# One fp32 product to a PSUM bank, wider token blocks and a shared weight ring in a mixture-of-experts stage

## The chip, the cores and the metric

The kernel runs on one NeuronCore of a Trainium2 chip. The metric is the device time of one execution in microseconds (us): the median of 3 runs before the change is 9032.1 us (9029.27 to 9032.78). The profile is of one execution that took 9036.42 us, of which 9034.7 us are the span between the first and the last instruction.

## The reference

Everything is fp32. A cross-attention of 4 x 1024 rows against 1024 columns comes first and takes the first 540 us; the change does not touch it. The rest is a mixture of experts over 4096 tokens of 1024 numbers, with 8 experts, each token going to two of them:

```python
topk_w, topk_idx = jax.lax.top_k(router_probs, TOP_K)          # TOP_K = 2
topk_w = topk_w / jnp.sum(topk_w, axis=-1, keepdims=True)
...
h = jax.lax.ragged_dot(x_rep_sort, w1, group_sizes)            # 1024 -> 3584
h = jax.nn.silu(h) * jax.lax.ragged_dot(x_rep_sort, w3, group_sizes)
out_sort = jax.lax.ragged_dot(h, w2, group_sizes)              # 3584 -> 1024
...
out = jnp.einsum('tkd,tk->td', out_rep, topk_w)
```

The router of the reference, evaluated on its inputs, sends 984, 991, 1080, 994, 1047, 1004, 1046 and 1046 tokens to the eight experts, 8192 in all.

## The kernel before, in words

The tokens of an expert are worked off in a *run* (`run`, L750) of `blocks` blocks of `width` tokens. The list RUNS (L22) has the allowed pairs; for each expert the smallest one that holds its tokens is chosen on the chip, and a loop over runs (L852) jumps through a switch to the code built for that pair. Here the eight runs are three blocks of 328 (once), 336 (three times), 352 (three times) and 360 tokens (once), 24 blocks and 8256 token places.

Every matrix product is one level of a Strassen-Winograd scheme: weights and tokens are cut in 2 x 2 quarters, and seven products p1 to p7 of half size replace eight. With n = width / 2, each product is a chain of matmuls with a 128 x 128 stationary weight and n moving columns, accumulated in PSUM. On an fp32 matmul TensorE executes two instructions, so two records in the profile are one matmul of the code. The seven products need sums of weight quarters (`weight_sums`, L580: four VectorE operations L585 to L588 on every loaded weight tile) and sums of token quarters ("factors").

- **First and second product** (w1 and w3, L769 to L797): 14 steps i2, each with a round of 28 matmuls for w1 and one for w3 (L781). After a round `combine` (L610) reads the seven results from PSUM on ScalarE and VectorE; then SiLU, the product of the two, and `token_sums` (L598), which makes the token factors of the third product once and keeps all seven in the tile `g` (14 x 7 x n).
- **Third product** (w2, L809 to L834): four quarters q of the 1024 output columns; in each, 14 steps of seven matmuls (L820). Weights come in four tiles of 8, 8, 6 and 6 rows of 128 (W2K). The seven results are combined, transposed back to token rows (`tokens_out`, L723, tile pt_y), scaled and added into `acc`, which holds rows gathered from the output; after the fourth quarter GpSimd scatters `acc` to the output with an indirect DMA (L736). The last block's fourth quarter is finished in the next run (`leftover`).
- **The next block's tokens** are gathered to `rows` by GpSimd (`load_rows`, L681), and transposed to `x` by TensorE in steps (`tokens_in`, L693, tile pt_h, copied from PSUM by ScalarE and VectorE in turn).

The steps of `tokens_in` and `tokens_out` stand in a list `late`, from which one is taken at fixed places between the matmuls. PSUM has eight banks of 512 fp32 columns: two products of n columns share a bank (BANK, L592), seven products take four banks, six banks serve them in turn, and two serve the transposes. Weight tiles are taken in turn from a pool of three (`wp`); the first two of the next run have buffers of their own, `w1a` and `w3a` with sums `s1a` (L661 to L663), loaded at the start of the last block's third product (`load_first`, L687).

TensorE executes in the order of the code (`manual_schedule`, L857). On the other engines a scheduler fixes the order when the program is built. Each engine, and SP (SyncE), which issues all the weight loads, works its own list strictly in order: an instruction that waits holds up everything behind it.

Of the kernel before, what the change touches and what calls it, by code (L numbers as in the profile page):

```python
# [18 lines left out]
P = 128  # L19
N = 512  # L20

RUNS = [(1, 192), (1, 376), (2, 288), (2, 376), (3, 288)]  # L22
RUNS += [(3, w) for w in range(320, 377, 8)]
# [10 lines left out]
def kernel(  # L34
# [493 lines left out]
    with ExitStack() as st:  # L528
        fst = st.enter_context(tc.tile_pool(name="fst", bufs=1))
        wp = st.enter_context(tc.tile_pool(name="wp", bufs=3))  # L530
        hp = st.enter_context(tc.tile_pool(name="hp", bufs=1))
        gp = st.enter_context(tc.tile_pool(name="gp", bufs=2))
        ip = st.enter_context(tc.tile_pool(name="ip", bufs=2))
        ps = st.enter_context(tc.tile_pool(name="ps", bufs=6, space=PSUM))
        pst = st.enter_context(tc.tile_pool(name="pst", bufs=2, space=PSUM))
# [4 lines left out]
        W2K = [8, 8, 6, 6]  # L540
        RT = 3
# [3 lines left out]
        XW = RT * P  # L545
        assert all(w // 2 <= NM and w <= XW for _, w in RUNS)


        T1, B11, B12, B21, B22, T2, T4 = range(7)
        T3 = B12  # L550
# [9 lines left out]
        def load(wf, ex, k0, kn, c0):  # L560
            t = wp.tile([P, KD, QW], F32, tag="w", name="wt")
            weights(t, wf, ex, k0, kn, c0)
            return t

        def factors(t, kn, halves, s):

            n = kn // 2
            if halves:
                v = t[:, :kn, :].rearrange("p (i h) c -> p i h c", h=2)
                lo, hi = v[:, :, 0, :], v[:, :, 1, :]  # L570
            else:
                lo, hi = t[:, :n, :], t[:, n:kn, :]
            s1, s2, s4 = (s[:, j, :n, :] for j in range(3))

            return dict(
                p1=lo[:, :, :P], p2=hi[:, :, :P], p3=s4, p4=hi[:, :, P:], p5=s1, p6=s2,
                p7=lo[:, :, P:],
            )

        def weight_sums(t, kn, halves, s=None):  # L580
            if s is None:
                s = wp.tile([P, 3, HK, P], F32, tag="s", name="ws")
            f = factors(t, kn, halves, s)
# [4 lines left out]
            nc.vector.tensor_tensor(a21, a11, a21, ALU.subtract)  # L588
            return f

        RIGHT = dict(p1=B11, p2=B21, p3=B22, p4=T4, p5=T1, p6=T2, p7=T3)
        BANK = dict(p1=(0, 0), p2=(1, 0), p6=(1, 1), p5=(2, 0), p7=(2, 1), p3=(3, 0), p4=(3, 1))  # L592
        ENDS = ["p1", "p6", "p7", "p4"]
# [4 lines left out]
        def token_sums(v, n):  # L598

            def two(a, b):  # L600
                return v[..., a : b + 1 : b - a, :]

            nc.vector.tensor_tensor(two(T1, T3), two(B12, B22), two(B11, B12), ALU.subtract)
            nc.vector.tensor_tensor(v[..., T2, :], v[..., B22, :], v[..., T1, :], ALU.subtract)
            nc.vector.tensor_tensor(v[..., T4, :], v[..., B21, :], v[..., T2, :], ALU.subtract)

        def banks():
            return [ps.tile([P, N], F32, tag="ps", name=f"ps{i}") for i in range(4)]

        def combine(pp, n, c, wide):  # L610

            def pair(t):
                return t[:, : 2 * n].rearrange("p (a b) -> p a b", b=n)

            def twice(v):
# [3 lines left out]
            nc.scalar.copy(p1s, pp[0][:, :n])  # L619
            nc.vector.tensor_tensor(pair(c), pair(pp[1]), twice(p1s), ALU.add)  # L620
            vu = gp.tile([P, 2, n], F32, tag="vu", name="vu")
            nc.vector.tensor_tensor(vu, pair(pp[2]), twice(c[:, n : 2 * n]), ALU.add)  # L622
            mid = c[:, n : 2 * wide - n].rearrange("p (a b) -> p a b", b=wide - n)[:, :, :n]
            nc.vector.tensor_tensor(mid, pair(pp[3]), vu, ALU.add)  # L624
            nc.vector.tensor_tensor(  # L625
                c[:, wide + n : wide + 2 * n], pp[2][:, :n], vu[:, 1, :], ALU.add
            )

# [30 lines left out]
        rd0 = fst.tile([P, RT], I32, name="rd0")  # L659
        rows = [fst.tile([P, D], F32, name=f"rows{s}") for s in range(RT)]  # L660
        w1a = fst.tile([P, KD, QW], F32, name="w1a")  # L661
        w3a = fst.tile([P, KD, QW], F32, name="w3a")
        s1a = fst.tile([P, 3, HK, P], F32, name="s1a")  # L663
# [6 lines left out]
        acc = [fst.tile([P, D], F32, name=f"acc{s}") for s in range(RT)]  # L670
        for a in acc:
            nc.gpsimd.memset(a, 0.0)
# [8 lines left out]
        def load_rows(s0):  # L681
            load_ids(ids0, s0)
            where_from(rd0, ids0)
            for s in range(RT):
                gather(rows[s], h_d, rd0, s, P)

        def load_first(i):  # L687
            ex = expert(i)
            load_rows(first_slot(i))
            weights(w1a, w1f, ex, 0, KD, 0)  # L690
            weights(w3a, w3f, ex, 0, KD, 0)

        def tokens_in():  # L693


            def step(s, h):
                pt = pst.tile([P, N], F32, tag="pt", name="pt_h")
                for k in range(HK):
                    nc.tensor.transpose(  # L699
                        pt[:, ts(k, P)], rows[s][:, ts(HK * h + k, P)], ident  # L700
                    )
                src = pt.rearrange("p (a b) -> p a b", b=P)
                dst = x[:, ds(HK * h, HK), ts(s, P)]
                if h % 2:
                    nc.vector.tensor_copy(dst, src)
                else:
                    nc.scalar.copy(dst, src)
# [14 lines left out]

        def tokens_out(ids, split, q, y):  # L723
# [3 lines left out]
            def step(s, r):  # L727
                pt = pst.tile([P, N], F32, tag="pt", name="pt_y")
                for d in range(2):
                    nc.tensor.transpose(pt[:r, ts(d, P)], yv[:, d, ds(s * P, r)], ident)  # L730
                part = acc[s][:r, ts(q, QW)]
                nc.vector.scalar_tensor_tensor(
                    part, pt[:r, :QW], ids.bitcast(F32)[:r, s, 1:2], part, ALU.mult, ALU.add
                )
                if q == DQ - 1:
# [3 lines left out]
                        in_=acc[s][:r, :],  # L739
# [7 lines left out]
        def leftover():  # L747
            return tokens_out(ids1, [P] * RT, DQ - 1, y1)

        def run(i, ex, s0, blocks, width):  # L750
            n = width // 2
            split = [min(P, width - c) for c in range(0, width, P)]

# [9 lines left out]
            for b in range(blocks):  # L763
                ids, rd = take_ids()
                last = b == blocks - 1
                if not last:
                    load_rows(s0 + (b + 1) * width)
                g = hp.tile([P, NI, 7, n], F32, tag="g", name="g")
                for i2 in range(NI):  # L769
                    cs = []  # L770
                    for wf, wa, tag in ((w1f, w1a, "c1"), (w3f, w3a, "c3")):
                        t = load(wf, ex, 0, KD, i2 * QW) if b or i2 else wa
                        if t is w1a:
                            left = factors(w1a, KD, False, s1a)
                        else:
                            left = weight_sums(t, KD, False)
                        pp = banks()
                        for p in ORDER if b or i2 else EARLY:
                            bk, half = BANK[p]
                            for k in range(HK):  # L780
                                nc.tensor.matmul(  # L781
                                    pp[bk][:, ts(half, n)], left[p][:, k, :],
                                    right[p][:, k, :],
# [8 lines left out]
                    nc.scalar.activation(c1, c1, AF.Silu)  # L792
                    nc.vector.tensor_tensor(
                        g[:, i2, B11 : B22 + 1, :].rearrange("p a b -> p (a b)"), c1, c3,
                        ALU.mult,
                    )
                    token_sums(g[:, i2, :, :], n)  # L797

                if last:
                    load_first(i + 1)  # L800
# [6 lines left out]
                for s, r in enumerate(split):  # L807
                    gather(acc[s][:r, :], of, rd, s, r)
                for q in range(DQ):  # L809
                    pp = banks()  # L810
                    i2 = 0
                    for kn in W2K:
                        t = load(w2f, ex, 2 * i2, kn, q * QW)
                        left = weight_sums(t, kn, True)
                        for k in range(kn // 2):
                            for p in ORDER:
                                bk, half = BANK[p]


                                nc.tensor.matmul(  # L820
                                    pp[bk][:, ts(half, n)], left[p][:, k, :],
                                    g[:, i2, RIGHT[p], :],
                                    start=(i2 == 0 and half == 0),
                                    stop=(i2 == NI - 1 and p in ENDS),
                                )
                            i2 += 1
                            if late and i2 > 1:
                                late.pop(0)()
                    if last and q == DQ - 1:
# [5 lines left out]
                    if q == 1:  # L835
                        late += tokens_in()

                        def sums():
                            nonlocal right
                            if last:  # L840
                                weight_sums(w1a, KD, False, s1a)
                            else:
                                right = token_factors(n)

                        late.append(sums)

        load_first(0)
        for step in tokens_in():
            step()
        weight_sums(w1a, KD, False, s1a)  # L850
# [38 lines left out]
```

## Time and profile before

| what | value |
|---|---|
| profiled execution | 9036.42 us, span 9034.7 us, mean granted TensorE clock 0.985 |
| median of 3 runs | 9032.1 us |
| TensorE matmuls busy | 98% of the span (last 37 of the 40 slices at 90% or more) |
| VectorE, ScalarE, GpSimd busy | 57%, 8%, 5% |
| weight loads | 848 of 1024 KB and 192 of 768 KB, and 9 each of w1a and w3a |
| DMA engines | mean share between 0.2 and 0.4, 137 GB/s |
| mixture of experts | from about 541 us to the end |

A row of instructions has: line, engine, operation, tiles written and read, shape; then its total busy time in us and the mean of one in ns; then how long its engine stood idle before it, and what ended that wait. In the chain of waits a row is: start, length, what filled it. In the DMA table the last number is the median time from issue to landing. TensorE's busy time alone does not tell whether it is at its peak, so the time from one instruction to the next is used below.

### The profile page before, as it was taken

The page shows a single profiled execution, that of the slowest core. Times are in us where ns is not written, and L with a number is a line of the kernel's source. Part 1 is how long each engine was busy: PE and PEld are TensorE (multiplying, and loading weights), DVE is VectorE, ACT ScalarE, POOL GpSimd, SP SyncE. Part 2 cuts the span into 40 slices and gives each one's busy share as a digit, 9 for nine tenths or more (in the row PEclk, how much of TensorE's full clock was granted, in tenths as well). Part 3 has the DMA queues.
Part 4 walks back from the last instruction along what each step waited for, and adds up shares of the span by engine and source line. Part 5 has one row for each costly group of instructions (what it writes and reads, how often), then busy time and mean ns, then how long its engine had stood idle before and what let it go on. Part 6 is the DMA issues. An engine that isn't in the chain of part 4 may idle for free. (4 is left out here: it accounts for less than half of the span.)

```text
span 9034.7 us, 139994 instructions
## 1 busy us (share of the span) xinstructions
PE 8818.7 (98%) x59458; PEld 8659.7 (96%) x59459; DVE 5115.4 (57%) x10062; ACT 698.7 (8%) x1527; POOL 423.7 (5%) x503
## 2 busy tenths in 40 slices
PE   8969999999999999999999999999999999999999
PEld 5569999999999999999999999999999999999999
DVE  5655655655645646556556556465565565555554
ACT  3310000000000000000000000000000000000000
POOL 2310000000000000000000000000000000000000
PEclk9979999999999999999999999999999999999999
DMA  3234444443433444344444434444443444434343
GB/s 133 109 118 142 145 145 134 149 150 128 162 131 119 144 135 139 129 136 143 143 134 141 144 121 141 143 132 150 137 151 131 133 138 136 141 131 142 126 139 126
DMA packets 1117375, 1236.40 MB, mean 137 GB/s; under 512 B 35552, under 2 KB 1077984, under 8 KB 1116576
## 3 DMA queue, kind: packets, MB, share of 16 engines
q1 hardware_dynamic: 1079424, 1114.54, 37.5%
q0 software_dynamic: 32656, 107.24, 3.3%
q8 instruction: 501, 8.21, 0.4%
q10 hardware_dynamic: 4496, 3.97, 0.1%
q14 instruction: 298, 2.44, 0.1%
HBM read 1155.26 MB, written 73.53 MB: 136 GB/s over the span
## 5 line engine op out<-in xcount | busy, mean ns | idle before, releaser
L781 PE MATMUL ps<-x,wt 128*128 128x168 f32 (+3 forms) x15744 | 2510.6, 309 | 0.0
L781 PEld LDWEIGHTS ps<-x,wt 128*128 128x128 f32 x15744 | 2351.8, 190 | 0.0
L820 PE MATMUL ps<-g,wt 128*128 128x168 f32 (+3 forms) x10752 | 2071.0, 309 | 0.0
L585 DVE TENSOR_TENSOR ws<-wt 128x512 f32<-128x512 f32 (+1 forms) x1040 | 693.7, 667 | 1991.4 <-DMA wt<-in_L_ffn_w_dram 1948.6
L820 PEld LDWEIGHTS ps<-g,wt 128*128 128x128 f32 x10752 | 1691.4, 190 | 0.0
L781 PE MATMUL ps<-xs,ws 128*128 128x168 f32 (+3 forms) x10624 | 1659.2, 309 | 0.0
L820 PE MATMUL ps<-g,ws 128*128 128x168 f32 (+3 forms) x8064 | 1615.3, 309 | 0.0
L781 PEld LDWEIGHTS ps<-xs,ws 128*128 128x128 f32 x10624 | 1579.0, 190 | 0.0
L820 PEld LDWEIGHTS ps<-g,ws 128*128 128x128 f32 x8064 | 1294.7, 190 | 0.0
L620 DVE TENSOR_TENSOR c<-ps,p1s 128x352 f32<-128x352 f32 (+3 forms) x672 | 346.6, 516 | 1099.9 <-PE ps L781 1066.5
L781 PE MATMUL ps<-x,ws 128*128 128x168 f32 (+3 forms) x5312 | 883.2, 309 | 0.0
L781 PE MATMUL ps<-xs,wt 128*128 128x168 f32 (+3 forms) x5248 | 872.6, 309 | 0.0
L781 PEld LDWEIGHTS ps<-x,ws 128*128 128x128 f32 x5312 | 804.0, 190 | 0.0
L781 PEld LDWEIGHTS ps<-xs,wt 128*128 128x128 f32 x5248 | 794.3, 190 | 0.0
L586 DVE TENSOR_TENSOR ws<-ws,wt 128x512 f32<-128x512 f32 (+1 forms) x1040 | 691.9, 665 | 28.5
L588 DVE TENSOR_TENSOR wt<-wt 128x512 f32<-128x512 f32 (+1 forms) x1040 | 684.8, 658 | 0.0
L587 DVE TENSOR_TENSOR ws<-wt,ws 128x512 f32<-128x512 f32 (+1 forms) x1040 | 684.0, 658 | 0.0
L619 ACT COPY p1s<-ps 128x168 f32<-128x168 f32 (+3 forms) x768 | 228.3, 297 | 4704.8 <-PE ps L781 2348.7
L792 ACT ACTIVATE c<-c 128x672 f32<-128x672 f32 (+3 forms) x336 | 261.5, 778 | 2604.3 <-DVE c L624 2583.1
L624 DVE TENSOR_TENSOR c<-ps,vu 128x352 f32<-128x352 f32 (+3 forms) x672 | 344.4, 512 | 72.7 <-PE ps L781 68.5
L622 DVE TENSOR_TENSOR vu<-ps,c 128x352 f32<-128x352 f32 (+3 forms) x672 | 342.1, 509 | 5.0 <-PE ps L781 4.8
L650 POOL DMA_INDIRECT rows<-h_d,rd x75 | 81.5, 1087 | 4869.7 <-issue 2405.9
(186 smaller groups left out, 3762.7 us busy)
## 6 DMA issues: line engine op xcount, KB each, us to landing
wt<-in_L_ffn_w_dram SPq DMA_DIRECT2D x848, 1024.0 KB, 4.9
wt<-in_L_ffn_w_dram SPq DMA_DIRECT2D x192, 768.0 KB, 4.6
xt<-in_x_dram SPq DMA_DIRECT2D x32, 512.0 KB, 4.3
out_dram<-x SPq DMA_DIRECT2D x32, 512.0 KB, 2.9
h_d<-hn SPq DMA_DIRECT2D x32, 512.0 KB, 2.6
w1a<-in_L_ffn_w_dram SPq DMA_DIRECT2D x9, 1024.0 KB
w3a<-in_L_ffn_w_dram SPq DMA_DIRECT2D x9, 1024.0 KB, 13.4
cx<-in_ctx_dram SPq DMA_DIRECT2D x4, 1024.0 KB, 9.5
```

The source lines that it names most:

```text
L585: nc.vector.tensor_tensor(f["p5"], a21, a22, ALU.add)
L586: nc.vector.tensor_tensor(f["p6"], f["p5"], a11, ALU.subtract)
L587: nc.vector.tensor_tensor(f["p3"], a12, f["p6"], ALU.subtract)
L588: nc.vector.tensor_tensor(a21, a11, a21, ALU.subtract)
L619: nc.scalar.copy(p1s, pp[0][:, :n])
L620: nc.vector.tensor_tensor(pair(c), pair(pp[1]), twice(p1s), ALU.add)
L622: nc.vector.tensor_tensor(vu, pair(pp[2]), twice(c[:, n : 2 * n]), ALU.add)
L624: nc.vector.tensor_tensor(mid, pair(pp[3]), vu, ALU.add)
L650: nc.gpsimd.indirect_dma_start(out=dst, out_offset=None, in_=src, in_offset=bass.IndirectOffsetOnAxis(ap=rd[:n, s : s + 1], axis=0),)
L781: nc.tensor.matmul(pp[bk][:, ts(half, n)], left[p][:, k, :], right[p][:, k, :], start=(k == 0), stop=(k == HK - 1),)
L792: nc.scalar.activation(c1, c1, AF.Silu)
L820: nc.tensor.matmul(pp[bk][:, ts(half, n)], left[p][:, k, :], g[:, i2, RIGHT[p], :], start=(i2 == 0 and half == 0), stop=(i2 == NI - 1 and ...
```

## The change

Runs have at most two blocks of at most 564 tokens, in steps of 4 per block: here one run each of 2 x 492, 496, 500, 504 and 540, and three of 2 x 524, that is 16 blocks and 8208 places. Since n is now up to 282, a product has a bank to itself: seven banks for one round (`ps1`, and three pairs `ps2`), one left for the transposes (`pst` has 1 buffer instead of 2). `g` keeps four of the seven factors; the other three are made anew in every quarter (`hidden_factors`, two VectorE operations for each of the 14 steps, in a pool `tp` of four). The weight tiles are three fixed buffers `w0`, `w1`, `w2` with sums `s0`, `s1`, `s2`, used strictly in turn, and the first two tiles of the next run lie in this ring too: they are loaded in the last quarter, after the third and the fourth of its five weight tiles. The last weight tile of a quarter runs its matmuls product by product instead of step by step. `acc` is gone: `rows` serves both as the gathered tokens and as the accumulator, the tokens are transposed in the first quarter, and each gather from the output follows the transposes of its rows. `load_rows` moves into the first product, i2 = 4. W2K is [4, 6, 6, 6, 6].

```diff
-RUNS = [(1, 192), (1, 376), (2, 288), (2, 376), (3, 288)]
-RUNS += [(3, w) for w in range(320, 377, 8)]
+RUNS = [(1, 192), (1, 376), (1, 564), (2, 376), (2, 432)]
+RUNS += [(2, w) for w in range(480, 565, 4)]
...
-        wp = st.enter_context(tc.tile_pool(name="wp", bufs=3))
+        tp = st.enter_context(tc.tile_pool(name="tp", bufs=4))
-        ps = st.enter_context(tc.tile_pool(name="ps", bufs=6, space=PSUM))
-        pst = st.enter_context(tc.tile_pool(name="pst", bufs=2, space=PSUM))
+        ps1 = st.enter_context(tc.tile_pool(name="ps1", bufs=1, space=PSUM))
+        ps2 = st.enter_context(tc.tile_pool(name="ps2", bufs=3, space=PSUM))
+        pst = st.enter_context(tc.tile_pool(name="pst", bufs=1, space=PSUM))
-        W2K = [8, 8, 6, 6]
-        RT = 3
+        W2K = [4, 6, 6, 6, 6]
+        WR = 3
+        ROWS = [P, P, P, P, P // 2]
+        RT = len(ROWS)
...
         def banks():
-            return [ps.tile([P, N], F32, tag="ps", name=f"ps{i}") for i in range(4)]
+            one = ps1.tile([P, N], F32, tag="ps1", name="ps1")
+            two = [ps2.tile([P, 2, N], F32, tag="ps2", name=f"ps2_{i}") for i in range(3)]
+            pp = dict(p1=one)
+            for t, (a, b) in zip(two, (("p2", "p6"), ("p5", "p7"), ("p3", "p4"))):
+                pp[a], pp[b] = t[:, 0, :], t[:, 1, :]
...
-            nc.vector.tensor_tensor(mid, pair(pp[3]), vu, ALU.add)
             nc.vector.tensor_tensor(
-                c[:, wide + n : wide + 2 * n], pp[2][:, :n], vu[:, 1, :], ALU.add
-            )
+                c[:, wide + n : wide + 2 * n], qb[:, 0, :n], vu[:, 1, :], ALU.add
+            )
+            nc.vector.tensor_tensor(mid, qc[:, :, :n], vu, ALU.add)
...
-        def load_first(i):
-            ex = expert(i)
-            load_rows(first_slot(i))
-            weights(w1a, w1f, ex, 0, KD, 0)
-            weights(w3a, w3f, ex, 0, KD, 0)
+        def load_first(i, j):
+
+            weights(wts_in[j], (w1f, w3f)[j], expert(i), 0, KD, 0)
...
+        def hidden_factors(v, n):
+
+            t = tp.tile([P, 3, n], F32, tag="t", name="t")
+            t2 = t[:, 0, :]
+            nc.vector.tensor_tensor(t2, v[:, B22, :], v[:, T1, :], ALU.subtract)
+            nc.vector.tensor_tensor(
+                t[:, 1:3, :], v[:, B11 : B21 + 1 : B21 - B11, :],
+                t2.unsqueeze(1).to_broadcast([P, 2, n]), ALU.subtract,
+            )
...
+                    if i2 == RT - 1:
+                        assert not late
+                        load_rows(first_slot(i + 1) if last else s0 + width)
...
-                for s, r in enumerate(split):
-                    gather(acc[s][:r, :], of, rd, s, r)
+                late += tokens_in(rows_of_out)
+                if not last:
+                    late.append(lambda: token_factors(n))
                 for q in range(DQ):
                     pp = banks()
                     i2 = 0
-                    for kn in W2K:
-                        t = load(w2f, ex, 2 * i2, kn, q * QW)
-                        left = weight_sums(t, kn, True)
...
+                    for u, kn in enumerate(W2K):
+                        j = load(w2f, 2 * i2, kn, q * QW)
+                        left = weight_sums(j, kn, True)
+                        todo = [
+                            (p, k) for k in range(kn // 2) for p in ORDER
+                        ] if u < len(W2K) - 1 else [
+                            (p, k) for p in ORDER for k in range(kn // 2)
+                        ]
+                        hid = [hidden_factors(g[:, i2 + k, :, :], n) for k in range(kn // 2)]
+                        for at_m, (p, k) in enumerate(todo):
+                            nc.tensor.matmul(
+                                pp[p][:, :n], left[p][:, k, :], hid[k][p],
+                                start=(i2 + k == 0), stop=(i2 + k == NI - 1),
+                            )
+                            if late and at_m % 7 == 6 and i2 + at_m // 7 > 0:
+                                late.pop(0)()
+                        i2 += kn // 2
+                        if last and q == DQ - 1 and u in (len(W2K) - 3, len(W2K) - 2):
+                            first = u - (len(W2K) - 3)
+                            assert j % WR == first
+                            load_first(i + 1, first)
+                            if first == 0:
+                                weight_sums(0, KD, False)
...
-                    if q == 1:
-                        late += tokens_in()
-
-                        def sums():
-                            nonlocal right
-                            if last:
-                                weight_sums(w1a, KD, False, s1a)
-                            else:
-                                right = token_factors(n)
-
-                        late.append(sums)
```

## The prediction

> **What bounds the kernel now.** I read the busy table first, then the chain of waits of the last run, then the timeline at a run's start, at its loads and at the kernel's end. Busy table, then a stage row (first product of the last run's first block: length, then PE, PE weight load, DVE, ACT and POOL busy, clock, DMA share, GB/s), then the chain (start, length, what):
>
> ```profile
> PE 8818.7 (98%) x59458; PEld 8659.7 (96%) x59459; DVE 5115.4 (57%) x10062; ACT 698.7 (8%) x1527; POOL 423.7 (5%) x503
> ```
> ```profile
> 7975.00:8183.80 208.80, 208.80 (x1402) 208.80 (x1401) 132.62 (x249) 16.69 (x38) 4.45 (x4) 1.00 0.41 135
> ```
> ```profile
> 7941.51 4.91 issue
> 7946.42 11.21 PE ps L781 x56
> ...
> 7966.43 8.36 PE ps L781 x56
> ...
> 7975.00 208.84 PE ps L781 x1400
> ...
> 8249.46 0.22 PE pt_y L730 x2
> ...
> 8254.08 0.44 PE pt_h L699 x4
> ```
>
> TensorE never stops inside a run: 208.84 / 1400 = 149.2 ns from one instruction to the next at n = 176. The block with n = 164 takes 1.95 us for 14, 139.3 ns. The slope is 0.83 ns a column, and 149.2 - 0.833 x 176 leaves 2.6 ns for each instruction. The only breaks are between runs: 10.46 us idle in the PE row of the timeline (4.91 of it "issue"), then 56 instructions in 11.21 us instead of 8.36, a loss of 2.85 us. So time is won by fewer columns or fewer instructions, and lost by whatever stops TensorE.
>
> **Gain on the stream.** A block has 14 x 2 x 28 + 4 x 14 x 7 = 1176 matmuls, 2352 instructions. Before: sum of n over 24 blocks 4128, so 2352 x (0.833 x 4128 + 24 x 2.6 ns) = 8238 us. After: sum 4104 over 16 blocks, 8142 us. **-96 us**, half from padding, half from the 2.6 ns.
>
> **Transposes.** Before, per block 6 x 0.44 + 12 x 0.22 = 5.3 us, x 24 = 127. After, 8 x 0.44 + 2 x about 0.24 (64 columns) + 20 x 0.22 = 8.4, x 16 = 134. **+8 us**.
>
> **Weight loads at the end of a run.** This is the step that decides. The order of SP's list in the built program is, in the last quarter of every run: tile 3 of w2 into w0, then the next run's w1 tile into w0, then tile 4 of w2 into w1, then the next run's w3 tile into w1, then tile 5 of w2 into w2. The load of the next w1 tile must wait until tile 3's matmuls, the readers of w0, are over; tile 4's load stands behind it although its own buffer has long been free. TensorE needs tile 4 at that very moment, so it waits for two loads, issued back to back. The same happens between tile 4 and tile 5. Before, the two tiles had buffers of their own and nothing stood behind a wait:
>
> ```profile
> wt<-in_L_ffn_w_dram SPq DMA_DIRECT2D x848, 1024.0 KB, 4.9
> wt<-in_L_ffn_w_dram SPq DMA_DIRECT2D x192, 768.0 KB, 4.6
> ```
> ```profile
> 8872.70 0.37 SPq L553 DMA_DIRECT2D w1a<-in_L_ffn_w_dram  x1
> 8873.25 1.13 SPq L553 DMA_DIRECT2D w3a<-in_L_ffn_w_dram  x1
> ```
>
> The first load alone lands after 4.9 us. Queue 1's packets took 37.5% of 16 engines for 1,079,424 packets of about 1 KB: 50 ns each. The 1024 KB therefore hold the engines 64 x 50 = 3.2 us; the 768 KB behind them need 4.6 us of their own after that, less about 0.3 us of start that overlaps. Estimate 7.5 us (bounds: 4.6 if both ran side by side unhindered; 10.1, the median of three 1024 KB loads issued together at a run's start, beside gathers). VectorE's list has the four sums of the next w1 tile first (landing 4.9, sums 4 x 0.68 = 2.7: 7.6 us), then tile 4's first two sums (1.1 us): 8.7 us. TensorE can do p1 and p2 meanwhile, so this adds nothing at a slow start.
>
> Then the clock. The Trainium skill, "TensorE: Matmul & The Clock Gate", Part 1, has TensorE drop to half rate after about 3.4 us without work and run so for about 3.4 us of work, which I estimate from the page at 1.7 us lost per stop. The trace has 2.85 us after 10.5 us idle, and at the first run's start 16 + 8 instructions in 4.73 and 1.94 us instead of 2.39 and 1.28 after 6.0 us idle, 3.0 us:
>
> ```profile
> 562.85 4.73 PE L781 MATMUL ps<-x,w1a 128*128 128x164 f32 x16 [6.01 <-issue]
> 567.38 1.94 PE L781 MATMUL ps<-x,s1a 128*128 128x164 f32 x8
> ...
> 573.83 2.39 PE L781 MATMUL ps<-x,w3a 128*128 128x164 f32 x16
> ```
>
> I take 2.9: 7.5 + 2.9 = 10.4 us, twice in each of 8 runs: **+166 us** (by the page's price 16 x 9.2 = 147). Bounds: 16 x (5.2 + 1.7) = 110 and 16 x (10.1 + 3.0) = 210. The skill also speaks against the shared ring in general ("Trainium Kernel Development and Optimization", Best Practices: double-buffer so that DMA overlaps compute); without the overlap the rows above are the price.
>
> **One PSUM tile for the transposes.** Before there were two. In the first quarter a transpose step follows every seven matmuls (3.1 us at n = 262), and the next step may start only when its predecessor was copied out. VectorE's built order puts the copy of the eighth step behind the sums of the next quarter's first weight tile, and these wait for a load into w0, free only when the third tile's matmuls end; call that T. The 512 KB land near T + 4.9 beside the gathers. Then come four sums of 128x256 (0.42 each, between the rows 0.34 for 176 and 0.52 for 352 elements), two pairs of factors (0.43 + 0.70 each, from the same slope) and the copy (0.69): T + 9.5. TensorE is there at T + 0.44 + 6.2 + 0.44 = T + 7.1. It waits 2.4 to 2.9 us, 16 times: **+42 us**. Bounds: 16 x 1.2 = 19 (landing at 4.3, operations overlapping) and 16 x 4.1 = 66 (landing at 6.5). Steps behind other copies have at least 1 us to spare.
>
> **What costs nothing, and its cover.** VectorE in a quarter: sums 10.6, factors 14 x 1.13 = 15.8, combine 2.5, adding rows 2.4 (5 x 0.478): 31 us of TensorE's 44. It isn't the bound. At the seam of two quarters, bank pair p3/p4 must be read out before the next quarter's sixth matmul, 2.2 us after the last one; by the built order the read-out ends 1.3 to 1.7 us after it, so 0.5 to 0.9 us to spare; each further us late would cost 64 us over 64 seams. In the first product, 28 matmuls last 12.4 us and VectorE needs about 6 a round; each bank pair is read out several us ahead. In place of 24 x 44 loads there are 16 x 48, and a third of the weight sums goes: both were hidden, so nothing is won. The gathers moved to i2 = 4 have 200 us; the gathers from the output have 10 us or more before their first use. The breaks between runs stay at 10.5 + 2.85: same loop, same jump, 8 starts.
>
> **The two ends.** The last scatters wait for each other:
>
> ```profile
> 9020.67 1.01 POOL L736 DMA_INDIRECT out_dram<-acc,ids  x1 [138.94 <-DVE acc L732]
> 9025.31 0.99 POOL L736 DMA_INDIRECT out_dram<-acc,ids  x1 [3.62 <-DMA out_dram<-acc,ids]
> 9029.43 0.98 POOL L736 DMA_INDIRECT out_dram<-acc,ids  x1 [3.12 <-DMA out_dram<-acc,ids]
> ```
>
> Five in place of three: 2 x 4.4 = 9 us. At the start ten transpose steps through one tile, about 1.5 us each (0.85 transposing at the low clock, 0.65 copying), in place of six in 5.1 us: about 8. **+17 us** (10 to 25).
>
> **Sum**: -96 + 8 + 166 + 42 + 17 = +137 on the profiled execution's 9036.4: 9173. That execution is 4.3 above the median of the runs, so I predict 9170 us for the median, 1.5% slower. With every bound at its low end -96 + 8 + 110 + 19 + 10 = +51 (9083 for the median); at its high end -96 + 8 + 210 + 66 + 25 = +213, with 15 us for late seams +228 (9260).
>
> **Rivals.** (1) *Faster*: fewer blocks win after all, because the loads behind the wait cost little. Place: the two changes of weight tile in the last quarter. Without stops there and at the transposes: -96 + 8 + 17 = -71, 8961 us. For it: the stream's gain is sure. Against it: SP's list is strict, and a wait behind tile 3's last matmul can't be passed; the loads' 4.6 us alone, 16 times, is 74. It wins only if a stop costs less than 71 / 16 = 4.4 us with its clock, and the transposes nothing. 4%. (2) *Small stops*: both loads share the engines, land 5.2 us after issue, the clock recovers at the page's price, and the transposes wait half: -71 + 110 + 21 = +60, 9092. 14%. (3) *VectorE becomes the bound of the third product*: the factors made four times queue behind loads, and each of the 20 weight tiles of a block stops TensorE 0.5 us: +160, 9330. For it: it waits in strict order for loads, matmuls and PSUM; against it: 70% filled, and the factors are made a tile ahead. 8%. (4) The forecast as summed: 74%.
>
> A measurement of this kernel tells about 0.2%, 18 us, from no change. Faster 0.04 is rival 1; same 0.03 lies between rivals 1 and 2; slower 0.93. The range 9095 to 9260 leaves out rivals 1 and 3, and some of 2.
>
> **What the profile after would show.** Right: PE idle about 7.5 us twice in each run's last quarter, ended by a weight load, with slow matmuls after; SP's longest waits for a PE event in front of a w1 load; idle of about 2.6 us before one pt_h transpose in a block's first quarter, ended by a VectorE copy; 0.83 n + 2.6 ns per instruction elsewhere. Wrong: no PE idle there (rival 1), or many gaps of under 1 us ended by VectorE's factors or sums (rival 3); or a stream slower per column at n near 262 than at 176.

## The result, and the profile after

The changed kernel takes 9140.2 us (median of 4 runs, 9133.1 to 9141.7) where the kernel before took 9030.7 us on the same chip: a ratio of 1.0118, 95% interval 1.0105 to 1.0131. The profiled execution took 9141.7 us, its span is 9140.0 us; the span before was 9034.7, so there are 105.3 us to explain.

TensorE does less and stands more. First the busy row of the changed kernel, then the two largest rows of its table of waits on TensorE (what waited for what, us in total, times, longest):

```profile
PE 8781.5 (96%) x40734; PEld 7561.4 (83%) x40735; DVE 4824.7 (53%) x8784; ACT 666.3 (7%) x1169; POOL 449.3 (5%) x516
```
```profile
PE ps L843 <- DMA w<-in_L_ffn_w_dram: 127.9, 16, 8.8
PE ps L793 <- issue: 77.9, 8, 10.5
```

18,700 instructions are gone and TensorE is busy 37 us less. In their place stand 16 waits of the third product (L843) for a weight load, two in each of 8 runs, 127.9 us in all. The table of the kernel before has no such row. The 77.9 us are the breaks between runs, which were there before.

The chain of waits of the last run shows the undisturbed stream of a first product, and at its end both stops (start, length, what):

```profile
8100.85 284.44 PE ps L793 x1288
...
9070.20 6.20 PE ps L843 x28
...
9076.42 0.37 SPq L558
...
9076.99 6.95 DMA w<-in_L_ffn_w_dram
...
9083.99 11.85 PE ps L843 x42
...
9095.85 0.37 SPq L558
...
9096.42 6.98 DMA w<-in_L_ffn_w_dram
...
9103.44 12.35 PE ps L843 x42
```

The third tile's matmuls end at 9076.40; 0.02 us later SP issues the two loads that stood behind them, TensorE starts the fourth tile at 9083.99, and the same happens again at 9095.83. SP's two loads in the timeline, and the first 4.66 us after the stop, in which TensorE was granted half its clock (stretch, length, PE, PE weight load, DVE, ACT and POOL busy, clock, DMA share, GB/s):

```profile
9076.42 1.00 SPq L558 DMA_DIRECT2D w<-in_L_ffn_w_dram  x2
```
```profile
9083.99:9088.65 4.66, 4.66 (x11) 3.62 (x12) 2.37 (x5) 0.00 (x0) 0.00 (x0) 0.50 0.02 4
```

Twenty-eight instructions before the stop took 6.20 us, so 42 should take 9.30; they take 11.85 and 12.35. The stream ahead of them is as it was: 1288 instructions in 284.44 us are 220.8 ns each at n = 262, and 0.833 x 262 + 2.5 is 220.7.

### The profile page after: what moved, and what is told of

It reads as the page before. It is cut to its first block, busy times and chain, and to the rows that moved or that the text cites. A ratio compares the mean times of both kernels' runs of the same rounds, so it can differ in the third digit from the quotient of the medians.

```text
span 9140.0 us, 99350 instructions
## 1 busy us (share of the span) xinstructions
PE 8781.5 (96%) x40734; PEld 7561.4 (83%) x40735; DVE 4824.7 (53%) x8784; ACT 666.3 (7%) x1169; POOL 449.3 (5%) x516
## 5 line engine op out<-in xcount | busy, mean ns | idle before, releaser
L793 PE MATMUL ps<-x,w 128*128 128x262 f32 (+5 forms) x10752 | 2490.2, 381 | 78.6 <-issue 77.9
L793 PEld LDWEIGHTS ps<-x,w 128*128 128x128 f32 x10752 | 2044.9, 191 | 370.0 <-issue 80.8
L793 PE MATMUL ps<-xs,s 128*128 128x262 f32 (+5 forms) x7168 | 1625.9, 379 | 0.0
L793 PEld LDWEIGHTS ps<-xs,s 128*128 128x128 f32 x7168 | 1354.9, 189 | 195.1
L843 PE MATMUL ps<-g,w 128*128 128x262 f32 (+5 forms) x3584 | 932.0, 390 | 127.9 <-DMA w<-in_L_ffn_w_dram 127.9
L843 PE MATMUL ps<-g,s 128*128 128x262 f32 (+5 forms) x3584 | 1030.0, 380 | 0.1
L843 PE MATMUL ps<-t,w 128*128 128x262 f32 (+5 forms) x3584 | 1026.8, 380 | 0.0
L793 PE MATMUL ps<-xs,w 128*128 128x262 f32 (+5 forms) x3584 | 848.3, 379 | 0.0
L793 PE MATMUL ps<-x,s 128*128 128x262 f32 (+5 forms) x3584 | 848.2, 380 | 0.0
L843 PEld LDWEIGHTS ps<-g,w 128*128 128x128 f32 x3584 | 666.3, 195 | 215.9 <-DMA w<-in_L_ffn_w_dram 134.3
L843 PEld LDWEIGHTS ps<-g,s 128*128 128x128 f32 x3584 | 683.5, 191 | 96.9 <-DVE y L624 0.5
L843 PEld LDWEIGHTS ps<-t,w 128*128 128x128 f32 x3584 | 680.6, 190 | 97.1
L843 PE MATMUL ps<-t,s 128*128 128x262 f32 (+5 forms) x1792 | 517.0, 382 | 0.0
```

Source lines behind the costliest of these rows:

```text
L793: nc.tensor.matmul(pp[p][:, :n], left[p][:, k, :], right[p][:, k, :], start=(k == 0), stop=(k == HK - 1),)
L843: nc.tensor.matmul(pp[p][:, :n], left[p][:, k, :], hid[k][p], start=(i2 + k == 0), stop=(i2 + k == NI - 1),)
```

## The experiments

All ratios are to the kernel before, run on the same chip in the same rounds; its median was 9030.7 us beside the changed kernel, 9036.1 beside the next four kernels of the table and 9026.6 beside the last four. Differences between two kernels are therefore best taken from the ratios.

| kernel | us | ratio (95%) |
|---|---|---|
| changed kernel | 9140.2 | 1.0118 (1.0105 to 1.0131) |
| both pairs of loads exchanged | 8975.3 | 0.9935 (0.9922 to 0.9949) |
| the same, and start through separate banks | 8963.3 | 0.9923 (0.9909 to 0.9936) |
| second pair exchanged alone | 9052.2 | 1.0019 (1.0011 to 1.0027) |
| TensorE kept at work in the waits | 9118.7 | 1.0093 (1.0077 to 1.0108) |
| first w2 tile fetches six rows | 9130.1 | 1.0114 (1.0098 to 1.0129) |
| old runs in the new layout | 9270.4 | 1.0271 (1.0256 to 1.0285) |
| kernel before, runs in steps of 4 | 9007.6 | 0.9978 (0.9969 to 0.9987) |
| one token factor made twice | 9131.8 | 1.0117 (1.0101 to 1.0132) |

### Both pairs of loads exchanged

```diff
+        SWAP = (0, 1)
...
+                    early = None
                     for u, kn in enumerate(W2K):
-                        j = load(w2f, 2 * i2, kn, q * QW)
+                        if early is None:
+                            j = load(w2f, 2 * i2, kn, q * QW)
+                        else:
+                            j, early = early, None
...
+                            if first in SWAP:
+                                early = load(w2f, 2 * i2, W2K[u + 1], q * QW)
                             load_first(i + 1, first)
-                            if first == 0:
+                            if first == 0 and 0 not in SWAP:
+                                weight_sums(0, KD, False)
+                            if first == 1 and 0 in SWAP:
                                 weight_sums(0, KD, False)
```

The next w2 tile is asked for ahead of the next run's tile, and takes its load from `early` where there is one.

> In the last quarter of a run, tile 4 of w2 is asked for before the next run's w1 tile, and tile 5 before the next run's w3 tile, so that no load that TensorE needs at once stands behind a load that must wait for matmuls. The sums of the next w1 tile are made one tile later. Nothing else changes. Theory (the two stops at the end of a run are SP's strict list and nothing else, 7.6 us of waiting and about 2.85 us of slow clock each): both stops vanish, 16 x 10.4 = 166 us less than the changed kernel, about 8974 us, 0.6% faster than the kernel before. The fifth tile's load is still issued with the end of the third tile's matmuls, behind 1 MB for the next run, and lands 7.6 us later; its matmuls start 9.3 us later. Rival A (the engines of the DMA are the limit there: any 1 MB that is fetched meanwhile delays the tile): the stops shrink to 2 to 4 us, at most half is won, 9050 to 9090. Rival B (the wait only moves, to the next run's first matmuls, whose loads are asked for later): the time stays within 20 us of 9140.

Measured: 8975.3 us, 164.9 below the changed kernel. By the ratios, 1.0118 - 0.9935 of 9031, it is 165 too. The table of waits has no wait of the third product for a load, and the chain runs through the last quarter's end in one piece:

```profile
8921.38 3.09 PE ps L848 x14
8924.48 0.22 PE pt_y L739 x2
8924.69 24.75 PE ps L848 x112
8949.47 0.71 DVE y L625
```

112 instructions in 24.75 us are 221.0 ns each: neither a wait nor a slow clock is left. So the stops came from the order of SP's list: with the same loads in another order they are gone. Rival A falls: the fifth tile's load still follows 1 MB for the next run, but TensorE wants it 9.3 us after it is issued. Rival B falls: the first matmuls of the next run wait as long as before (about 10.3 us).

### The start through separate banks as well

```diff
-                pt = pst.tile([P, 4, P], F32, tag="pt", name="pt_h")
+                if halves is None:
+                    pt = pst.tile([P, 4, P], F32, tag="pt", name="pt_h")
+                else:
+                    pt = halves.pop(0).rearrange("p (k c) -> p k c", c=P)
```

Before the first run only, `halves` holds ten banks of the products' PSUM tiles.

> The last run's edit on the order of loads, and the ten transposing steps before the first run each write a PSUM bank of their own, in place of ten turns through one tile. Theory: 8974 as for the order of loads alone, and 6 to 8 us less from the start (the ten steps took 1.8 us each, 1.1 of transposing and 0.7 of waiting for the copy; only the 0.7 goes): about 8967, faster than both kernels. Rival (the rows' gathers set the pace of the ten steps, not the tile): 8974, no gain beside the other edit.

Measured: 8963.3 us, 12 less than with the exchanged loads alone, and 0.77% faster than the kernel before. The timeline of TensorE at the start:

```profile
549.14 5.07 PE L696 MATMUL ps<-ident,rows 128*128 128x128 f32 x24 [54.63 <-DMA rows<-h_d,rd]
...
555.39 1.06 PE L696 MATMUL ps<-ident,rows 128*128 128x128 f32 x8 [1.19 <-DMA rows<-h_d,rd]
...
562.96 5.67 PE L797 MATMUL ps<-x,w 128*128 128x246 f32 x16 [5.45 <-issue]
```

From the first transpose to the first matmul it is 13.8 us; in the changed kernel it was 22.6, with the exchanged loads alone 22.4, in the kernel before 11.1. So 8.6 of the 12 us are seen to be this edit's. The rest lies ahead of it: in this trace the transposes began at 549.1 us, with the exchanged loads alone at 553.9, and most of that difference is there already in the routing stage, which is the same code. The rival is half right: near the end of the ten steps a gather is what TensorE waits for, but only 1.2 us.

### The second pair alone

The same edit with `SWAP = (1,)`: only the second pair is exchanged, and the sums stay as in the changed kernel.

> Only the second of the two pairs of loads is exchanged: tile 5 of w2 is asked for before the next run's w3 tile, tile 4 still stands behind the next run's w1 tile. Theory (each of the two stops has its own load that waits ahead of it): the first stop stays, 7.6 us of waiting and about 3 us of slow clock, the second goes: 8 x 10.4 = 83 us less, about 9057. Rival B (a load that waits holds up all that follows, whatever the order; the wait moves): about 9140. Rival A (the amount fetched at that time counts): three loads together after tile 3 make the first stop longer, to 10 us or more, and the gain is about 60.

Measured: 9052.2 us, 88 below the changed kernel. One kind of stop is left (table of waits):

```profile
PE ps L848 <- DMA w<-in_L_ffn_w_dram: 60.3, 8, 8.0
```

8 x 7.5 us of waiting: no longer than before, although three loads leave together. So each stop has its own cause in SP's list, and the second was the dearer: 88 / 8 = 11.0 us, against (165 - 88) / 8 = 9.6 for the first. The timeline of the changed kernel has the same difference: the first wait of a run is 7.3 to 7.6 us, the second 8.5 to 8.8 in seven runs of eight (7.6 in the last).

### TensorE kept at work in the waits

```diff
                             load_first(i + 1, first)
                             if first == 0:
                                 weight_sums(0, KD, False)
+                            pt = pst.tile([P, 4, P], F32, tag="pt", name="pt_d")
+                            for d in range(60):
+                                nc.tensor.transpose(pt[:, d % 4, :], ident, ident)
```

> The changed kernel, and in each of the two waits at a run's end TensorE makes 60 transposes of the identity (about 6.6 us) that nobody reads; the results are as before. The loads and the waits stay. Theory (2.6 to 3.1 us of each stop are the clock, slow because TensorE stood still): 42 matmul instructions take 9.3 us after the wait in place of 11.9 and 12.4, 16 x 2.85 = 46 us less, about 9095. Rival (the slow matmuls after a stop come from late sums on VectorE, which the 7.6 us do not show, or from the weight loads): no change, 9140. The idle time of TensorE in front of the fourth and fifth tile should shrink to about 1 us in both cases, as the transposes fill it.

Measured: 9118.7 us, 22 less, not 46. Timeline of TensorE around both stops of the last run, first in the changed kernel, then here:

```profile
9083.99 2.12 PE L843 MATMUL ps<-g,w 128*128 128x262 f32 x4 [7.60 <-DMA w<-in_L_ffn_w_dram]
...
9103.44 5.61 PE L843 MATMUL ps<-g,w 128*128 128x262 f32 x12 [7.62 <-DMA w<-in_L_ffn_w_dram]
```
```profile
9058.64 6.71 PE L858 MATMUL pt_d<-ident 128*128 128x128 f32 x60
9066.09 1.15 PE L843 MATMUL ps<-g,w 128*128 128x262 f32 x4 [0.74 <-DMA w<-in_L_ffn_w_dram]
9067.61 0.71 PE L843 MATMUL ps<-t,s 128*128 128x262 f32 x2 [0.37 <-DVE s L586]
...
9085.03 2.92 PE L843 MATMUL ps<-g,w 128*128 128x262 f32 x12 [2.21 <-DMA w<-in_L_ffn_w_dram]
```

The mechanism holds: the first four instructions take 1.15 us in place of 2.12 and the first twelve 2.92 in place of 5.61. The rival falls, since loads and sums are as they were. Half the gain goes elsewhere. The clock's whole loss is smaller than I took: over the 16 stops of the changed kernel, from first matmul to last matmul of each tile less 42 x (0.833 n + 2.5 ns), it is 2.27 us at a first stop and 2.55 at a second, 38.6 us in all, not 46. The transposes and what is left of the waits add up to 16 x 6.7 + 28.9 = 136 us against 127.9, mostly because four of the eight first loads came 1.3 us later. Seven times TensorE then waited for VectorE's second sum (2.9 us in all); before, the slow clock lay over that wait. And in four of the 16 stops (three second ones and one first) the first twelve instructions still took 4.2 to 4.6 us after 2.0 to 2.3 us of idle time, while eight other stops with as much idle time lost nothing; four times 1.7 us is another 7. With 7 for the smaller loss, 8 for the transposes and 3 for the sums that makes 25, where 24 are missing.

The granted clock of the trace tells the four from the eight. It is either full or half, and it changes only on a grid of 3.41 us: every stretch of one clock is a whole multiple of that long. A step of the grid at a stop that lost nothing, then two neighbouring steps at one that did (columns as above, PE busy first after the length, the clock ahead of the last two numbers):

```profile
1554.56:1557.97 3.41, 1.44 (x14) 1.20 (x11) 2.04 (x4) 0.00 (x0) 0.00 (x0) 1.00 0.49 159
...
2588.80:2592.21 3.41, 1.38 (x12) 1.12 (x10) 2.48 (x4) 0.00 (x0) 0.00 (x0) 1.00 0.36 116
2592.21:2595.62 3.41, 3.41 (x9) 2.38 (x8) 2.06 (x5) 0.00 (x0) 0.00 (x0) 0.50 0.00 0
```

In the four stops TensorE was busy for 1.16 to 1.38 of the 3.41 us of the step before the clock went to half. In the twelve others no step has less than 1.44 us of work (where the idle time is as long, it is divided between two steps), and the clock stays full. So in this trace it is not the length of the idle time that decides, but how much of it falls into one step.

### The first w2 tile fetches six rows

```diff
-                    weights(wts_in[loads % WR], wf, ex, k0, kn, c0)
+                    weights(wts_in[loads % WR], wf, ex, k0, max(kn, 6), c0)
```

> The first w2 tile of each quarter fetches six rows of 128 and uses four, as before; so its load (768 KB) overwrites everything that the third tile's last step still reads. The forecast had 42 us because it let the 512 KB wait for the third tile's end. In the changed kernel's trace they were issued one step (3.5 us) earlier. Theory (what counts is whether the rows that are overwritten are still to be read, not the buffer's name): here the load is issued at the third tile's end, 3 to 3.5 us later than in the changed kernel. VectorE's built order then has the eighth copy ahead of these sums, so nothing waits for it: 9140, within 15. Rival (a buffer is freed as a whole, and the early issue has another reason): no difference in the place of the issue. The 42 us themselves can't come back here, since the copy no longer stands behind the sums.

Measured: 9130.1 us, ratio 1.0114: no difference. But the load moved. First the changed kernel, a block's first quarter (transpose step by step, SP's load, VectorE's sum and copy), then this one:

```profile
8937.47 0.60 PE L692 MATMUL pt_h<-ident,rows 128*128 128x128 f32 x4
8937.67 0.37 SPq L558 DMA_DIRECT2D w<-in_L_ffn_w_dram  x1
...
8941.24 0.42 DVE L585 TENSOR_TENSOR s<-w 128x256 f32<-128x256 f32 x1 [1.79 <-DMA w<-in_L_ffn_w_dram]
...
8944.54 0.60 PE L692 MATMUL pt_h<-ident,rows 128*128 128x128 f32 x4
...
8945.82 0.68 DVE L697 COPY x<-pt_h 128x512 f32<-128x512 f32 x1
```
```profile
8929.98 0.60 PE L692 MATMUL pt_h<-ident,rows 128*128 128x128 f32 x4
8930.17 0.37 SPq L558 DMA_DIRECT2D w<-in_L_ffn_w_dram  x1
...
8934.80 0.68 DVE L697 COPY x<-pt_h 128x512 f32<-128x512 f32 x1
8935.89 0.43 DVE L585 TENSOR_TENSOR s<-w 128x256 f32<-128x256 f32 x1 [0.41 <-DMA w<-in_L_ffn_w_dram]
```

In the changed kernel the load is issued beside the sixth transpose step, one step ahead of the third tile's end; here beside the seventh, at its end. So in this kernel a load waits for the readers of the rows that it overwrites: four rows of w0 are free when the tile's second step is through, six only after its third. The eighth copy stands behind the sums in the first list and ahead of them in the second: the order in which VectorE's work is built follows the time at which the load can start.

### Old runs in the new layout

```diff
-RUNS = [(1, 192), (1, 376), (1, 564), (2, 376), (2, 432)]
-RUNS += [(2, w) for w in range(480, 565, 4)]
+RUNS = [(1, 192), (1, 376), (2, 288), (2, 376), (3, 288)]
+RUNS += [(3, w) for w in range(320, 377, 8)]
...
-        ROWS = [P, P, P, P, P // 2]
+        ROWS = [P, P, P]
```

A run's third block takes in the tokens of its second again, which leaves the amount of work as it is.

> The changed kernel with the runs of the kernel before (up to three blocks of at most 376 tokens, steps of 8; three row tiles): the layout without the larger blocks. Theory: the stream is that of the kernel before, the stops at the ends of the 8 runs stay at 10.3 us each, 16 x 10.3 = 165, and the transposes through one tile at the start cost about 3: 9030 + 168, about 9200, ratio 1.019. Rival 3 of the forecast (VectorE bounds the third product) at its worst place: at n = 176 a quarter lasts 29.2 us, and VectorE has 10.6 of sums + about 11.5 of factors + 1.9 of read-out + 1.4 of rows, 25.4 of 29.2, waiting for PSUM and loads in strict order besides. If each of the 20 tiles of a block stops TensorE 0.5 us, 24 x 20 x 0.5 = 240 more: 9440.

Measured: 9270.4 us, 244 more than before: some 75 above the theory, far below the rival. Its waits on TensorE:

```profile
PE ps L843 <- DMA w<-in_L_ffn_w_dram: 126.4, 16, 8.7
PE ps L793 <- DVE c L621: 20.4, 19, 2.3
PE ps L843 <- DVE y L624: 9.7, 45, 0.2
```

The stops are the same size. What is new is a wait of the first product for a read-out of VectorE (20.4 us, 19 times in 24 blocks), and waits at the seams of two quarters. Summed over the whole trace outside the slow clock, what each interval between two instructions has above 0.833 n + 2.5 ns makes 26 us in the first product and 38 in the third: 64 of the 75 us. In the first product it is not VectorE that is short of time. In all 19 cases it had itself stood 4.5 to 6.7 us waiting for a weight load, and the read-out stands behind that load's sums in its list. One of the 19, VectorE first, then TensorE:

```profile
605.15 0.69 DVE L585 TENSOR_TENSOR s<-w 128x512 f32<-128x512 f32 x1 [5.57 <-DMA w<-in_L_ffn_w_dram]
...
607.97 1.35 PE L793 MATMUL ps<-xs,s 128*128 128x164 f32 x8 [1.19 <-DVE c L621]
```

At the seams the read-out stands between sums and factors in VectorE's list and comes about 0.4 us late. So what rival 3 named does happen in this layout at n = 176, but at the seams and behind late loads, not at every tile.

### The kernel before, in steps of 4

```diff
-RUNS += [(3, w) for w in range(320, 377, 8)]
+RUNS += [(3, w) for w in range(320, 377, 4)]
```

> The kernel before, with its three-block runs in steps of 4 tokens in place of 8 (padding alone). Sum of n over the 24 blocks falls from 4128 to 4116 (8256 places to 8232). Theory (each instruction costs 0.833 ns a column): 2352 x 0.833 x 12 = 23.5 us less, about 9007 where the kernel before takes 9030.7, ratio 0.9974. Rival (the padding is paid elsewhere, or widths that are no multiples of 8 cost something in reading): no change.

Measured: ratio 0.9978 (0.9969 to 0.9987), 20 us of 9031: the interval holds the 23.5. Padding costs what the slope per column says, and this part of the change needs nothing of the rest.

### One token factor made twice

```diff
             nc.vector.tensor_tensor(t2, v[:, B22, :], v[:, T1, :], ALU.subtract)
+            nc.vector.tensor_tensor(t2, v[:, B22, :], v[:, T1, :], ALU.subtract)
```

> The changed kernel with the first token factor of the third product made twice (same result): 14 more operations of about 0.43 us a quarter, 6 us, so that VectorE has 37 of TensorE's 44 us; 64 x 6 = 385 us more work for VectorE in all. Theory (VectorE has room in the third product, rival 3 is far off): 0 to 15 us more, from seams where its read-out comes later, 9140 to 9155. Rival 3 (VectorE is at its limit there through its waits, not its busy time): a third or more of the 385 us shows, 9270 or above.

Measured: 9131.8 us, ratio 1.0117. VectorE's busy row and the waits on TensorE:

```profile
PE 8772.2 (96%) x40734; PEld 7554.8 (83%) x40735; DVE 5155.3 (56%) x9680; ACT 666.5 (7%) x1169; POOL 435.0 (5%) x516
```
```profile
PE ps L844 <- DMA w<-in_L_ffn_w_dram: 126.5, 16, 8.7
```

VectorE's 331 us of additional work (5155.3 in place of 4824.7) cost nothing. At n near 262 rival 3 is far off.

## Why the prediction was right, and where it was not

The forecast was 9170 us with +137 on the profiled execution; measured are 9140 and +105. Term by term:

**Stream, -96: right.** 220.8 ns an instruction at n = 262 is the slope and, within 0.1 ns, the intercept of the forecast (with 2.5 ns it makes -94), and the padding's half of it was found in the kernel before alone.

**Stops, +166: right as a sum, and in part by luck.** Taking both away brought 165. The parts were a little off and made up for each other: 127.9 / 16 = 8.0 us of waiting in place of 7.5, since a second load lands about 1.1 us later than a first, and 38.6 / 16 = 2.4 us of clock in place of 2.9. The Trainium skill ("TensorE: Matmul & The Clock Gate", Part 1) has half the rate for some 3.4 us of work after a stop, an estimate of 1.7 us; it would have given 16 x 9.7 = 155 with the measured waits. In the trace the half clock lasts 3.3 to 5.7 us after TensorE starts again, in all 16 stops. The 2.9 was read at two starts of runs; over all eight starts of the kernel before the same reading gives 2.4 to 3.0 us, over those of the changed kernel 1.7 to 3.1. So it depends on where on the grid of the clock TensorE starts again, and two cases were too few for a mean.

**Transposes, +8: 14.** From start to start the transposes and what they delay take 139.7 us in place of 125.8. Each of the two half-size steps of a block (64 rows) costs TensorE about 0.6 us, where I had 0.24.

**One PSUM tile for the transposes, +42: wrong, nothing.** The table of waits of the changed kernel:

```profile
PE pt_h L692 <- ACT x L701: 3.2, 5, 0.7
PE pt_h L692 <- DVE x L697: 3.1, 4, 0.8
```

TensorE waits for copies nine times, 0.5 to 0.8 us each, and all nine are at the start of the stage; the 2.6 us in a block's first quarter are nowhere. The step that failed is "these wait for a load into w0, free only when the third tile's matmuls end". The load is 512 KB, four rows of w0, and was issued 3.5 us before that end; it landed after 3.6 us, where I had 4.9. The sums start at 8941.24, with the end of the third tile's matmuls, in place of 4.9 us after it. The eighth copy ends at 8946.50, and TensorE starts the ninth step at 8948.16, 1.7 us later. Issued at the tile's end in the same order of VectorE's list, the load would have landed at 8944.8; with 4.15 us of work from the sums to the copy (5.26 less 1.11 of waiting) the copy would have ended at 8948.9, about 0.8 us too late. So even with the old rule the term was 16 x 0.8 = 13 us by these times, an estimate, and not 42. At the run's end the rule of the forecast gives the right time, since the next run's loads have all eight rows and overwrite what the last step still reads. A sign was in what I had: the built order puts the copy behind those sums, and when the load is made late the order turns. The cost in the old order could not be brought about, so it is argued from these times and not measured.

**The two ends, +17: right, 18.6.** From the first transpose to the first matmul it is 22.6 us in place of 11.1, 11.5 more where I had 8: a full-size step takes 1.8 us and not 1.5. After the last matmul it is 24.2 us in place of 17.1, 7.1 more where I had 9: scatters stand 4.1 us apart. The start before, then after:

```profile
551.76 4.26 PE L699 MATMUL pt_h<-ident,rows 128*128 128x128 f32 x20 [51.53 <-DMA w3a<-in_L_ffn_w_dram]
```
```profile
554.95 1.09 PE L692 MATMUL pt_h<-ident,rows 128*128 128x128 f32 x4 [54.49 <-DMA w<-in_L_ffn_w_dram]
...
577.57 2.80 PE L793 MATMUL ps<-x,w 128*128 128x246 f32 x6 [6.01 <-issue]
```

**The breaks between runs, 0: 3.5 us less.** The seven breaks take 71.9 us of idle time in place of 73.5, and over the eight starts the first 56 instructions lose 19.2 us in place of 21.2. Nothing in the change aims at that; the loss differs from start to start with the grid of the clock, as at the stops.

The terms as measured make -94 + 14 + 166 + 0 + 19 - 3.5 = 101; 3 more lie ahead of the stage (the transposes began at 554.95, not 551.76). That is 104 of 105.3. The forecast's +137 was 32 too high: 42 were not paid, and the smaller terms together came to 10 more than forecast.

Of the rivals, the first was nearest to being made true by a change of order: without the stops the changed kernel would have been 8975, where I had 8961 for it. In this layout the larger blocks are worth more than I counted: the old runs have a ratio of 1.0271 and the new ones 1.0118, some 138 us less, where the forecast's terms for stream, transposes and ends make -71. The rest is about the 64 us that the old runs lose in this layout to late read-outs; the longer matmuls leave time for them. The gain of the change was real, 0.65% or 59 us with all its other costs paid, and was spent on two stops a run.

## What to carry to other kernels

When buffers are shared in a ring, read the queue's own list at each change of phase: a load that must wait for matmuls must not stand in front of one that TensorE needs as soon as they end. Put the needed load first; here two exchanged pairs of loads were worth 165 us and turned a slower kernel into a faster one. And when you ask when a buffer becomes free, ask it for the rows that the next load overwrites, not for the buffer.

## What the runs showed that I had not expected

Two loads issued together (1024 KB, then 768 KB) make TensorE wait 7.3 to 7.6 us at a run's first stop and 8.5 to 8.8 at its second, in seven runs of eight, with the same sizes and the same order; in the kernel with the busy waits four of the eight first stops were late by the same 1.3 us. The DMA records show what goes with it. A first stop of the changed kernel, then the second stop of the same run, by queue (packets, MB, share of 16 engines):

```profile
q1 hardware_dynamic: 1824, 1.84, 77.4%
```
```profile
q1 hardware_dynamic: 1824, 1.84, 64.6%
q14 instruction: 2, 0.02, 0.5%
```

The weight packets are the same, but in the late stop two packets of a queue that the profile calls "instruction" run among them, 8 KB and here 0.37 us each, where a weight packet takes 0.05. It is so in all five traces that have both stops (changed kernel, busy waits, six rows, old runs, factor made twice). Every late stop has two such packets or one of 16 KB (1.0 to 1.2 us), every other stop none or, in the last run, a single one of 8 KB. That this delays the last weight packets is likely and not shown: no run moved those packets.

After 7.3 to 8.8 us without work 42 matmul instructions lose 1.9 to 3.1 us, and an idle time of 2.2 us costs 1.7 us or nothing. Both follow the grid of the granted clock: the loss depends on where the idle time begins and ends on it.
